# A selective-scan and expert kernel on one core: further rows of longer blocks finished later, the last block in one piece, the first two chunks begun with the first tokens

## The chip, the cores and the metric

The kernel runs on one core of a Trainium2 chip (trn2). The metric is the device time of one execution in microseconds; where several executions were taken, the median. Engines are named as the profile names them: PE (TensorE; PEld its weight loads), DVE (VectorE), ACT (ScalarE), POOL (GpSimd), SP (SyncE, which issues DMAs).

## The reference, cut to what matters

One layer over 4096 tokens of 256 features: a Mamba-like mixer, a layer norm, a mixture of eight experts of which each token uses one, and another layer norm.

```
xz = x @ W_in                                  # 256 -> 2 x 512
convolved = silu(conv4(xz[:, :512]) + conv_b)  # depthwise, 4 taps, causal
x_dbl = convolved @ W_x                        # step size, B (16), C (16)
h[t] = exp(delta*A) * h[t-1] + delta*B*convolved[:, :16]   # scan over tokens
y = (sum(h*C) + convolved*D_param) * silu(xz[:, 512:])
x1 = layernorm(x + y @ W_out)
e = argmax(x1 @ Wr.T + br)                     # one of 8 experts per token
out = layernorm(x1 + relu(x1 @ W1[e].T + b1[e]) @ W2[e].T + b2[e])
```

Everything is float32.

## The kernel before

**First stage.** The tokens go in eight chunks of 512 (loop over `k` at the end of `mamba_moe`). For a chunk, `project(i, c)` (L740) is called for c = 0 to 7: it multiplies 128 columns of W_in (the tile `win`) with the chunk's tokens (`xTb`, features on partitions) into a PSUM bank `pm`, two matmuls over the two halves of the features. ACT evicts it: for c below 4 as `xc` and as `acc` (the first tap with its bias), and DVE adds three more taps (`taps`, L733, L736); silu gives `cv`. For c of 4 to 7 silu gives the gate `sg`. Between the projections of a chunk stand steps of the chunks before: `gauge`, `gauge_out`, `scan`, `gate`, `look`, `look_out`, `project_out`, `choose`, `rank`, `place`. These end in x1, written to DRAM (`x1d`), and in lists that sort the tokens by expert.

**The first DMAs.** Chunk 0's tokens come in two halves of 256 (`first = TB // 2`, L155). For each half SP loads the first 128 features, ACT's queue the other 128 (L162, L163); behind each half SP loads columns of `win` with `columns` (L159): 0 to 127 after the first half, 128 to 511 after the second, 512 to 1023 later (L169). Behind them on SP's queue stand the router weights `wr` (L173), the next chunk's tokens (L142) and smaller weights (`load_later`, L183). In `project(0, 0)` the products are made for the two token halves apart, so that the first can begin early; every other `project` takes 512 tokens at once. PE first turns an identity twelve times (L202), with nothing to compute. `router_weights` (L468), behind `project(0, 2)`, multiplies `wr` with ones into `pw` (L471); DVE makes `mean` of it (L476) and takes it from `wr` (L477), which the router's products `prx` (L894) then use.

**Second stage.** `blocks()` (L693) is a generator over 32 blocks of 128 tokens of one expert; the loop calls `expert(n)` to take n quarters of a block into PE's order, at first between steps of the first stage, then alone. A block `b` has a row gather (`xg`, by `prefetch`, two blocks ahead) and, where the expert changes, a weight load (`we`, 128 x 4360, three buffers), both indirect DMAs of POOL (L502, L520). Then `turn` (L543) transposes the rows into `xgT`; `hidden(b, 0)` and `hidden(b, 1)` (L562) make 8 x 128 hidden features: products `ph` (L577), then bias and relu into `hT`, the first half by ACT (L586), the second by DVE (L588); `close(b, 0)` and `close(b, 1)` (L592) make the output products `pe` (L628) from `hT`. `finish(b)` (L647) adds the rows and the output bias (`xs`, L605, then `r`, L650), and `layernorm` (L251) makes `y`: bn_stats (L256), bn_aggr (L258), square root on ACT (L260), reciprocal (L261), scale (L262). `scatter(b)` (L661) writes the rows of `y` to the output with an indirect DMA of POOL (L663), called in the next block's turn.

**Longer blocks.** Blocks 17, 20, 23, 26 and 29 (`LONG`) take 32, 32, 32, 64 and 64 further rows of their expert (`more_of`). The hidden products run over 160 or 192 columns; for the outputs of the further rows `close(b, 1)` has products of its own, `pf` (L639), split over 4 or 2 groups of partitions. `finish(b)` then does for them what it does for the main rows: `xs` (L656), the sum of the groups (L658), and `layernorm` with the names `stf`, `mvf`, `sdf`; all these rows lie in the tile called `long`. `scatter(b)` writes main and further rows one after the other.

**The last block.** For b = 31 `close` makes the 256 output columns in two halves of 128: all eight products for columns 0 to 127, then sum (L621) and statistics (L622) of that half, then the same for the other, both in one PSUM bank `pe`.

**Seldom blocks.** A loop for up to seven blocks beyond 32 (`seldom`, L671) stands behind block 28 and is skipped when not needed; gathers and scatters of its rows (`seldom`) are always issued by POOL.

**What sets the order.** PE's order is the order written here (`manual_schedule`). The other engines' order is made by a scheduler from the dependences and its own estimates, except where `issue_after` pins a step. A DMA on SP's or ACT's queue takes one of eight semaphores in turn and waits for the DMA that held it before.

Of the kernel before, what the change touches and what calls it, by code (L numbers as in the profile page):

```python
# [37 lines left out]
F32 = mybir.dt.float32  # L38
# [4 lines left out]
ALU = mybir.AluOpType  # L43
# [4 lines left out]
P = 128  # L48
# [3 lines left out]
TB = 512  # L52
# [47 lines left out]
def mamba_moe(  # L100
# [57 lines left out]
    def columns(at):  # L158
        nc.sync.dma_start(win[:, :, at], W_in[:, at].rearrange("(c p) n -> p c n", p=P))  # L159

    for at in (slice(0, first), slice(first, TB)):
        nc.sync.dma_start(st[0]["xTb"][:, 0, at], xT[0:P, at])  # L162
        nc.scalar.dma_start(st[0]["xTb"][:, 1, at], xT[P : 2 * P, at])  # L163
        columns(slice(0, P) if at.start == 0 else slice(P, DI))
    cw = const.tile([P, CC, KC], F32, name="cw")
    nc.scalar.dma_start(cw, conv_w.rearrange("(c p) k -> p c k", p=P))
    cb = const.tile([P, CC], F32, name="cb")
# [80 lines left out]
        allow_small_or_imprecise_dtypes=True,  # L248
    )

    def layernorm(pool, rows, done, name, st=None):  # L251

        n = rows.shape[0]
        if st is None:
            st = pool.tile([P, 6], F32, tag="st", name=f"st{name}")[0:n, :]
            nc.vector.bn_stats(st, rows)  # L256
        mv = pool.tile([P, 2], F32, tag="mv", name=f"mv{name}")[0:n, :]
        nc.vector.bn_aggr(mv, st)  # L258
        sd = pool.tile([P, 1], F32, tag="sd", name=f"sd{name}")[0:n, :]
        nc.scalar.activation(sd, mv[:, 1:2], AF.Sqrt, bias=eps[0:n, :])  # L260
        nc.vector.reciprocal(sd, sd)  # L261
        nc.vector.tensor_scalar(done, rows, mv[:, 0:1], sd, ALU.subtract, ALU.mult)  # L262
# [232 lines left out]
    xgs, wes, turned, hid, last, open_, ys = {}, {}, {}, {}, {}, {}, {}  # L495


    xgf, openf, yf, ends_, wide_, xss, seldom_in, halves = {}, {}, {}, {}, {}, {}, [], []
    current = 0

    def gather(to, rows, at):
# [90 lines left out]
    def close(b, half):  # L592
        we, hT = wes[b], hid[b]
        if half == 0:
            open_[b] = bank("o", f"pe{b}")
        py = open_[b]

        def out_weights(fc):
            return we[:, O2 + fc * D : O2 + (fc + 1) * D]

        def add_rows():
            xss[b] = m2.tile([P, D], F32, tag="xs", name=f"xs{b}")

            with tc.issue_after(last[b].ins):
                nc.vector.tensor_tensor(xss[b], xgs[b], we[:, OC : OC + D], ALU.add)  # L605

        if b == SURE - 1:


            at = slice(half * D // 2, (half + 1) * D // 2)  # L610
            for fc in range(FC):
                nc.tensor.matmul(
                    py[:, at], lhsT=hT[:, fc, :], rhs=out_weights(fc)[:, at],
                    start=(fc == 0), stop=(fc == FC - 1),
                )
            if half == 0:
                add_rows()
                halves.append(m2.tile([P, D], F32, tag="r", name=f"r{b}"))
                halves.append(a2.tile([P, 2, 6], F32, tag="sta", name=f"st{b}"))
            r, sts = halves  # L620
            nc.vector.tensor_tensor(r[:, at], py[:, at], xss[b][:, at], ALU.add)  # L621
            nc.vector.bn_stats(sts[:, half, :], r[:, at])  # L622
            if half == 1:
                ys[b] = m2.tile([P, D], F32, tag="y", name=f"y{b}")
                layernorm(m2, r, ys[b], f"m{b}", sts)
            return
        for fc in range(half * FC // 2, (half + 1) * FC // 2):
            nc.tensor.matmul(  # L628
                py[:, 0:D], lhsT=hT[:, fc, 0:P], rhs=out_weights(fc),
                start=(fc == 0), stop=(fc == FC - 1),  # L630
            )
# [11 lines left out]
        add_rows()  # L643
        if b != SELDOM:
            finish(b)

    def finish(b):  # L647
        we, py, xs = wes[b], open_[b], xss[b]
        r = m2.tile([P, D], F32, tag="r", name=f"r{b}")
        nc.vector.tensor_tensor(r, py[:, 0:D], xs, ALU.add)  # L650
        ys[b] = m2.tile([P, D], F32, tag="y", name=f"y{b}")
        layernorm(m2, r, ys[b], f"m{b}")
        if b in LONG:
            m = more_of(b)
            xs, r, yf[b] = (ends_[b][0:m, n * D : (n + 1) * D] for n in (1, 2, 3))
            nc.vector.tensor_tensor(xs, xgf[b], we[0:m, OC : OC + D], ALU.add)  # L656
            for g in range(0, P, m):
                nc.vector.tensor_tensor(r, openf[b][g : g + m, 0:D], r if g else xs, ALU.add)  # L658
            layernorm(m2, r, yf[b], f"f{b}")

    def scatter(b):  # L661
        for rows, at in ((ys[b], index[b][1]), *(((yf[b], further[b][0 : more_of(b), :]),) if b in LONG else ())):
# [70 lines left out]
    def taps(i, c):  # L733
        acc, xc = st[i]["acc", c], st[i]["xc"]
        for k in range(KC - 1):
            nc.vector.scalar_tensor_tensor(  # L736
                acc, xc[:, c, k : k + TB], cw[:, c, k : k + 1], acc, ALU.mult, ALU.add
            )

    def project(i, c):  # L740
# [10 lines left out]
        pm = bank("mm", f"pm{i}_{c}")  # L751

        for at in (slice(0, first), slice(first, TB)) if i == c == 0 else (slice(0, TB),):
            for dc in range(DC):
                nc.tensor.matmul(  # L755
                    pm[:, at], lhsT=win[:, dc, c * P : (c + 1) * P], rhs=xTb[:, dc, at],
                    start=(dc == 0), stop=(dc == DC - 1),
                )
        if c >= CC:
            evicted = nc.scalar.activation(sg[:, c - CC, :], pm, AF.Silu)  # L760
        else:
            nc.scalar.copy(xc[:, c, KC - 1 :], pm)  # L762
            acc = a3.tile([P, TB], F32, tag="acc", name=f"acc{i}_{c}")
            evicted = nc.scalar.activation(  # L764
                acc, pm, AF.Identity, scale=cw[:, c, KC - 1 : KC], bias=cb[:, c : c + 1]
            )
            s["acc", c] = acc
            if c < CC - 1:
                taps(i, c)
        if ("acc", c - 2) in s:  # L770

            with tc.issue_after(evicted.ins):
                nc.scalar.activation(cv[:, c - 2, :], s["acc", c - 2], AF.Silu)
        if c == CC and i + 1 < NB:

            after = st[i + 1]["xc"] = a2.tile(
                [P, CC, KC - 1 + TB], F32, tag="xc", name=f"xc{i + 1}"
            )
            nc.gpsimd.tensor_copy(after[:, :, 0 : KC - 1], xc[:, :, TB : TB + KC - 1])
# [428 lines left out]
```

## Time and profile before

| | us |
|---|---|
| median of three runs | 487.88 |
| lowest, highest of them | 486.55, 489.39 |
| the profiled execution | 486.12 |
| its span in the profile | 484.4 |
| PE busy in it | 471.3 |
| DVE, ACT, POOL busy | 340.3, 224.0, 185.9 |
| HBM read and written | 87.45 MB, 9.54 MB |

The 1.7 us between the profiled execution and its span lie outside the instructions. The first stage's products run from 4.6 us; from 345 us on only blocks of the second stage are left; the last block's products begin at 470.4 us, and the last scatter is issued at 480.5 us. The granted PE clock is 0.996 of full speed over the span.

How to read the rows: a timeline row has the start in us from the span's start, the length, the engine (a q behind it: its queue of issues), the line, the operation, the tiles written and read, the shape, how many instructions were merged, and in brackets the idle time of the engine before it with what ended it. A busy PE is not a PE at its peak, since ends of matmuls are modelled from starts. Each f32 matmul appears as two records.

### The profile page before, as it was taken

Reading aid. Unit: us, or ns where it says so; the run is one execution under the profiler, and the core shown is the slowest. Engines: PE = TensorE matmul, PEld = TensorE weight load, DVE = VectorE, ACT = ScalarE, POOL = GpSimd, SP = SyncE. Lnnn points to the kernel's source line nnn. Section 1 sums busy time; section 2 is a strip of 40 time slices with the busy share of each in tenths; the row PEclk is TensorE's granted clock in tenths of the full one; section 3 lists DMA queues with packets and bytes.
Section 4 is the critical chain, followed back from the end, with each engine's and each line's share of the span. In section 5 each row is a group of like instructions: output and inputs, shape, how many; then the busy total and the mean of one; then the engine's idle time right before and its main releaser. Section 6 shows DMA issues by size and latency. Waiting matters only on the chain. (4 is left out here: it accounts for less than half of the span.)

```text
span 484.4 us, 7580 instructions
## 1 busy us (share of the span) xinstructions
PE 471.3 (97%) x2618; PEld 352.9 (73%) x2618; DVE 340.3 (70%) x1117; ACT 224.0 (46%) x453; POOL 185.9 (38%) x194
## 2 busy tenths in 40 slices
PE   8999999999999999999999999999999999999984
PEld 5444555546464676777898999999989898889874
DVE  2587969798998997877799779445464645555343
ACT  3777768878878865848443132212111112122111
POOL 2001212444437454241514332535344456644621
PEclk9999999999999999999999999999999999999998
DMA  7501012130407918414677767999874399769700
GB/s 226 171 2 45 0 45 87 43 88 0 132 1 295 391 42 283 158 50 175 184 271 269 278 215 267 387 354 343 344 281 162 87 350 283 229 219 336 275 16 22
DMA packets 23049, 89.65 MB, mean 185 GB/s; under 512 B 4898, under 2 KB 14629, under 8 KB 19298
## 3 DMA queue, kind: packets, MB, share of 16 engines
q0 software_dynamic: 8672, 74.38, 42.2%
q1 hardware_dynamic: 13378, 14.50, 9.5%
q8 instruction: 21, 0.34, 0.3%
q10 hardware_dynamic: 960, 0.27, 0.3%
q14 instruction: 18, 0.15, 0.1%
HBM read 87.45 MB, written 9.54 MB: 200 GB/s over the span
## 5 line engine op out<-in xcount | busy, mean ns | idle before, releaser
L755 PE MATMUL pm<-xTb,win 128*128 128x512 f32 (+1 forms) x260 | 121.3, 597 | 0.2 <-DMA win<-in_W_in 0.2
L577 PEld LDWEIGHTS ph<-xgT,we 128*128 128x128 f32 x864 | 100.9, 192 | 6.3 <-issue 2.8
L577 PE MATMUL ph<-xgT,we 128*128 128x128 f32 x864 | 103.4, 276 | 0.6 <-issue 0.6
L628 PE MATMUL pe<-we,hT 128*128 128x256 f32 x416 | 96.1, 381 | 1.4 <-ACT hT L586 1.0
L628 PEld LDWEIGHTS pe<-we,hT 128*128 128x128 f32 x416 | 76.7, 190 | 11.9 <-ACT hT L586 1.2
L736 DVE SCALAR_TENSOR_TENSOR acc<-xc,cw,acc 128x512 f32<-128x512 f32 x96 | 72.9, 780 | 16.0 <-ACT acc L764 15.6
L755 PEld LDWEIGHTS pm<-xTb,win 128*128 128x128 f32 x260 | 47.6, 192 | 47.0 <-issue 40.9
L260 ACT ACTIVATE sdm<-mvm,eps 128x1 f32<-128x1 f32 x32 | 9.5, 296 | 143.7 <-DVE mvm L258 118.7
L520 POOL DMA_INDIRECT we<-in_experts,widx x32 | 33.7, 1054 | 90.5 <-DVE r L650 25.3
L921 PE MATMUL po<-wout,sg 128*128 128x264 f32 x256 | 64.1, 392 | 0.0
L885 POOL TENSOR_TENSOR sg<-cv,sg 128x512 f32<-128x512 f32 x22 | 32.8, 1495 | 59.3 <-DVE cv L880 45.9
L921 PEld LDWEIGHTS po<-wout,sg 128*128 128x128 f32 x256 | 46.1, 190 | 10.1 <-issue 2.9
L663 POOL DMA_INDIRECT out<-y,tidx x32 | 32.8, 1024 | 35.8 <-DVE y L262 23.4
L588 DVE TENSOR_SCALAR hT<-ph,we 128x128 f32<-128x128 f32 x108 | 31.4, 342 | 20.3 <-issue 8.8
L650 DVE TENSOR_TENSOR r<-pe,xs 128x256 f32<-128x256 f32 x31 | 13.1, 422 | 44.2 <-PE pe L628 37.7
L502 POOL DMA_INDIRECT xg<-x1d,tidx x32 | 32.1, 1004 | 31.0 <-DVE xd L811 7.5
L586 ACT ACTIVATE hT<-ph,we 128x128 f32<-128x128 f32 x108 | 30.7, 367 | 21.1 <-PE ph L577 14.3
L1009 POOL TENSOR_SCALAR rowh<-lrow,row,code 128x256 f16<-128x256 bf16 x20 | 26.0, 1308 | 27.2 <-DVE row L1001 26.0
L880 DVE SCALAR_TENSOR_TENSOR cv<-cv,dp,py 128x256 f32<-128x256 f32 x64 | 28.6, 471 | 3.4 <-PE py L873 3.4
L760 ACT ACTIVATE sg<-pm 128x512 f32<-128x512 f32 x32 | 19.0, 595 | 18.4 <-PE pm L755 16.0
L762 ACT COPY xc<-pm 128x512 f32<-128x512 f32 x32 | 18.6, 582 | 18.0 <-PE pm L755 17.8
L764 ACT ACTIVATE acc<-pm,cb,cw 128x512 f32<-128x512 f32 x32 | 25.1, 784 | 0.0
(224 smaller groups left out, 619.4 us busy)
## 6 DMA issues: line engine op xcount, KB each, us to landing
xb<-in_x SPq DMA_DIRECT2D x8, 512.0 KB, 6.2
x1d<-x SPq DMA_DIRECT2D x8, 512.0 KB, 6.0
xTb<-in_xT SPq DMA_DIRECT2D x7, 512.0 KB, 6.1
win<-in_W_in SPq DMA_DIRECT2D x1, 512.0 KB
we<-in_W_outT SPq DMA_DIRECT2D x1, 512.0 KB
wout<-in_W_out SPq DMA_DIRECT2D x1, 512.0 KB
we<-in_experts,widx POOLq DMA_INDIRECT x32
xg<-x1d,tidx POOLq DMA_INDIRECT x32
```

Of the source, the lines that this page charges most:

```text
L502: nc.gpsimd.indirect_dma_start(out=to, out_offset=None, in_=x1d[0:rows, :], in_offset=bass.IndirectOffsetOnAxis(ap=at, axis=0),)
L520: nc.gpsimd.indirect_dma_start(out=wes[n][:, :], out_offset=None, in_=experts, in_offset=bass.IndirectOffsetOnAxis(ap=weights[n], axis=0), ...
L577: nc.tensor.matmul(ph[:, n * w : (n + 1) * w], lhsT=we[:, at : at + P], rhs=xgT[:, dc * w : (dc + 1) * w], start=(dc == 0), stop=(dc == DC ...
L586: nc.scalar.activation(hT[:, fc, :], ph[:, n * w : (n + 1) * w], AF.Relu, bias=bias)
L588: last[b] = nc.vector.tensor_scalar(hT[:, fc, :], ph[:, n * w : (n + 1) * w], bias, 0.0, ALU.add, ALU.max)
L628: nc.tensor.matmul(py[:, 0:D], lhsT=hT[:, fc, 0:P], rhs=out_weights(fc), start=(fc == 0), stop=(fc == FC - 1),)
L663: moved = nc.gpsimd.indirect_dma_start(out=out, out_offset=bass.IndirectOffsetOnAxis(ap=at, axis=0), in_=rows, in_offset=None, bounds_chec ...
L736: nc.vector.scalar_tensor_tensor(acc, xc[:, c, k : k + TB], cw[:, c, k : k + 1], acc, ALU.mult, ALU.add)
L755: nc.tensor.matmul(pm[:, at], lhsT=win[:, dc, c * P : (c + 1) * P], rhs=xTb[:, dc, at], start=(dc == 0), stop=(dc == DC - 1),)
L880: nc.vector.scalar_tensor_tensor(cv[:, c, at], cv[:, c, at], dp[:, c : c + 1], py[:, 0 : TB // 2], ALU.mult, ALU.add,)
L885: eng.tensor_tensor(sg[:, c, :], cv[:, c, :], sg[:, c, :], ALU.mult)
L921: nc.tensor.matmul(po[:, 0 : D + NE], lhsT=sg[:, c, j * P : (j + 1) * P], rhs=wout[:, c, :], start=(c == 0), stop=(c == CC - 1),)
```

## The change

Three edits.

1. `columns(slice(0, P))` and `columns(slice(P, 2 * P))` are both loaded behind the first token half, and columns 256 to 511 behind the second. `project(0, 0)` makes the products of the first 256 tokens for chunks of columns 0 and 1 into two banks, then those of the second 256 tokens for columns 0; `project(0, 1)` those of the second 256 tokens for columns 1.
2. `finish` keeps the main rows alone. The further rows' `xs` is written in `close(b, 1)`, and the rest is a new function `finish_further`, called for block b - 1 behind `hidden(b, 1)`. Their scatter is called one block later, behind the next block's main scatter.
3. The case of the last block goes: it is closed and finished as every other, in one piece of 256 columns.

```diff
         nc.scalar.dma_start(st[0]["xTb"][:, 1, at], xT[P : 2 * P, at])
-        columns(slice(0, P) if at.start == 0 else slice(P, DI))
+        if at.start == 0:
+            columns(slice(0, P))
+            columns(slice(P, 2 * P))
+    columns(slice(2 * P, DI))
...
-        if b == SURE - 1:
-            at = slice(half * D // 2, (half + 1) * D // 2)
-            for fc in range(FC):
-                nc.tensor.matmul(
-                    py[:, at], lhsT=hT[:, fc, :], rhs=out_weights(fc)[:, at],
-                    start=(fc == 0), stop=(fc == FC - 1),
-                )
-            if half == 0:
-                add_rows()
...
-            nc.vector.tensor_tensor(r[:, at], py[:, at], xss[b][:, at], ALU.add)
-            nc.vector.bn_stats(sts[:, half, :], r[:, at])
-            if half == 1:
-                ys[b] = m2.tile([P, D], F32, tag="y", name=f"y{b}")
-                layernorm(m2, r, ys[b], f"m{b}", sts)
-            return
...
+        if b in LONG:
+            nc.vector.tensor_tensor(
+                ends_[b][0 : more_of(b), D : 2 * D], xgf[b], we[0 : more_of(b), OC : OC + D],
+                ALU.add,
+            )
...
+    def finish_further(b):
         if b in LONG:
             m = more_of(b)
             xs, r, yf[b] = (ends_[b][0:m, n * D : (n + 1) * D] for n in (1, 2, 3))
-            nc.vector.tensor_tensor(xs, xgf[b], we[0:m, OC : OC + D], ALU.add)
             for g in range(0, P, m):
                 nc.vector.tensor_tensor(r, openf[b][g : g + m, 0:D], r if g else xs, ALU.add)
             layernorm(m2, r, yf[b], f"f{b}")
...
             if 0 < b:
                 scatter(b - 1)
+                scatter(b - 2, False)
...
             hidden(b, 1)
+            finish_further(b - 1)
             yield
...
+        if i == 0 and c < 2:
+            if c == 0:
+                for n in range(2):
+                    products(n, slice(0, first))
+            products(c, slice(first, TB))
+        else:
+            products(c, slice(0, TB))
+        pm = banks.pop(c)
```

`products(c, at)` is the pair of matmuls of `project` for one chunk of columns and the tokens `at`; `scatter(b, False)` writes the further rows of block b alone.

More of the change, by code (lines that the diff above doesn't have):

```diff
@@ L249, in mamba_moe, with layernorm @@
     )
-    def layernorm(pool, rows, done, name, st=None):
+    def layernorm(pool, rows, done, name):
         n = rows.shape[0]
-        if st is None:
-            st = pool.tile([P, 6], F32, tag="st", name=f"st{name}")[0:n, :]
-            nc.vector.bn_stats(st, rows)
+        st = pool.tile([P, 6], F32, tag="st", name=f"st{name}")[0:n, :]
+        nc.vector.bn_stats(st, rows)
         mv = pool.tile([P, 2], F32, tag="mv", name=f"mv{name}")[0:n, :]
@@ L495, in mamba_moe @@
     xgs, wes, turned, hid, last, open_, ys = {}, {}, {}, {}, {}, {}, {}
-    xgf, openf, yf, ends_, wide_, xss, seldom_in, halves = {}, {}, {}, {}, {}, {}, [], []
+    xgf, openf, yf, ends_, wide_, xss, seldom_in = {}, {}, {}, {}, {}, {}, []
     current = 0
@@ L599, in out_weights @@
             return we[:, O2 + fc * D : O2 + (fc + 1) * D]
[L601 to L605, printed above, removed]
-        if b == SURE - 1:
-            at = slice(half * D // 2, (half + 1) * D // 2)
-            for fc in range(FC):
-                nc.tensor.matmul(
-                    py[:, at], lhsT=hT[:, fc, :], rhs=out_weights(fc)[:, at],
-                    start=(fc == 0), stop=(fc == FC - 1),
-                )
-            if half == 0:
-                add_rows()
[L618 to L621, printed above, removed]
-            nc.vector.bn_stats(sts[:, half, :], r[:, at])
-            if half == 1:
-                ys[b] = m2.tile([P, D], F32, tag="y", name=f"y{b}")
-                layernorm(m2, r, ys[b], f"m{b}", sts)
-            return
         for fc in range(half * FC // 2, (half + 1) * FC // 2):
@@ L642, in close @@
                 )
-        add_rows()
+        xss[b] = m2.tile([P, D], F32, tag="xs", name=f"xs{b}")
+        with tc.issue_after(last[b].ins):
+            nc.vector.tensor_tensor(xss[b], xgs[b], we[:, OC : OC + D], ALU.add)
+        if b in LONG:
[3 more added lines that the diff above has]
+            )
         if b != SELDOM:
@@ L659, in finish, with scatter @@
             layernorm(m2, r, yf[b], f"f{b}")
-    def scatter(b):
-        for rows, at in ((ys[b], index[b][1]), *(((yf[b], further[b][0 : more_of(b), :]),) if b in LONG else ())):
+    def scatter(b, main=True):
+        rows_at = ((ys[b], index[b][1]),) if main else ()
+        if not main and b in LONG:
+            rows_at = ((yf[b], further[b][0 : more_of(b), :]),)
+        for rows, at in rows_at:
             moved = nc.gpsimd.indirect_dma_start(
@@ L738, in taps @@
             )
+    banks = {}
     def project(i, c):
@@ L750, in project, with products @@
         xc, cv, sg = s["xc"], s["cv"], s["sg"]
-        pm = bank("mm", f"pm{i}_{c}")
-        for at in (slice(0, first), slice(first, TB)) if i == c == 0 else (slice(0, TB),):
+        def products(c, at):
+            if c not in banks:
+                banks[c] = bank("mm", f"pm{i}_{c}")
             for dc in range(DC):
                 nc.tensor.matmul(
-                    pm[:, at], lhsT=win[:, dc, c * P : (c + 1) * P], rhs=xTb[:, dc, at],
+                    banks[c][:, at], lhsT=win[:, dc, c * P : (c + 1) * P], rhs=xTb[:, dc, at],
                     start=(dc == 0), stop=(dc == DC - 1),
                 )
+        if i == 0 and c < 2:
[6 more added lines that the diff above has]
+        pm = banks.pop(c)
         if c >= CC:
```

## The prediction

> **What bounds the kernel now.** I read first the busy shares and the split by stretches of the span, then who TensorE waited for, then the timeline at the two ends and around the last longer block.
>
> ```profile
> PE 471.3 (97%) x2618; PEld 352.9 (73%) x2618; DVE 340.3 (70%) x1117; ACT 224.0 (46%) x453; POOL 185.9 (38%) x194
> ```
>
> TensorE (PE) is the bound: 471.3 of 484.4 us. Between 24 and 345 us it is busy 318.83 of 321 us, between 345 and 458 us 111.89 of 113. So only three places can give anything: the first 12 us, the last 20, and the few waits left between. The list of TensorE's waits (line, releaser, us in total, times, longest):
>
> ```profile
> PE idle L202 <- POOL ident masks.py:199: 1.6, 1, 1.6
> PE pe L628 <- ACT hT L586: 1.0, 1, 1.0
> ...
> PE ph L577 <- issue: 0.6, 2, 0.4
> ...
> PE pe L628 <- DVE hT L588: 0.4, 1, 0.4
> ...
> PE pe L612 <- DVE r L621: 0.4, 1, 0.4
> ```
>
> All its idle time sums to about 7 us. Of this the change can touch: 1.0 + 0.6 us after block 29 (a longer block), 0.4 us after block 23 (the longer block whose products end at 407 us), 0.4 us in the last block, and what the start loses.
>
> **Part 1: the first two chunks.** Weight loads (PEld) show the start best (start us, length, what, idle before):
>
> ```profile
> 4.57 1.35 PEld L755 LDWEIGHTS pm<-xTb,win 128*128 128x128 f32 x4 [0.52 <-issue]
> 6.66 0.73 PEld L755 LDWEIGHTS pm<-xTb,win 128*128 128x128 f32 x4 [0.73 <-DMA xTb<-in_xT]
> 7.75 0.30 PEld L755 LDWEIGHTS pm<-xTb,win 128*128 128x128 f32 x2 [0.37 <-DMA win<-in_W_in]
> 8.29 0.19 PEld L755 LDWEIGHTS pm<-xTb,win 128*128 128x128 f32 x1 [0.24 <-issue]
> ```
>
> An f32 matmul is two records (I say passes). Chunk 0's first 256 tokens take four passes from 4.60 (4.60, 5.16, 5.58, 6.01 in the trace, 0.43 apart), then TensorE waits for the second 256 tokens until 6.66, then four passes 0.22 apart, then a wait for the further columns until 7.75; chunk 2 begins at 9.58. Pass spacings once running: 0.216 us at 256 columns, 0.43 at 512 (rows 8.29, 8.72, 9.15), so four passes of 256 and two of 512 cost the same; the extra weight loads hide (PEld 73%).
>
> After the change chunk 1's first 256 tokens fill the first wait. They need columns 128 to 255, a DMA now of its own, third on SP's queue. If it has landed: first half of chunk 0 over at 6.3 (four passes of 0.43), chunk 1's half 0.32 + 3 x 0.216 = 0.97 to 7.27 (0.32 is the first step after 6.66), two second halves of 4 x 0.216 to 9.00: chunk 2 starts at 9.00 instead of 9.58, -0.58. From the other side: that DMA now stands in the queue where the second 256 tokens stood, released at 6.66; then chunk 2 starts at 6.66 + 0.97 + 1.73 = 9.36, -0.22. If the second tokens, now one 128 KB DMA later, come only when the further columns came (7.75): 7.75 + 1.73 = 9.48, -0.10. I take **-0.45**, near the first: the 128 KB column DMA of now takes 3.2 us from issue to landing, and one issued 0.45 later would be there at 4.9.
>
> What else moves on SP's queue: one issue more (0.4 to 0.5 each), so everything behind stands later. The remaining 256 columns must wait until the first DMA of their semaphore is done, so are issued at about 3.6 (now 2.23); now's 384 KB took 7.75 - 2.23 = 5.5, so by 9.1 at the latest, just when chunk 2 needs them at 9.00; their 256 KB should be sooner. The router weights (wr) slip about 0.45.
>
> [...]
>
> VectorE's order changes too: the operation "mean", which waits for the products with wr, moves from behind seven taps to behind the first:
>
> ```profile
> 9.20 1.54 DVE L736 SCALAR_TENSOR_TENSOR acc<-xc,cw,acc 128x512 f32<-128x512 f32 x2 [7.78 <-ACT acc L764]
> ...
> 15.06 0.16 DVE L476 TENSOR_SCALAR mean<-pw 128x8 f32<-128x8 f32 x1
> ...
> 15.85 0.17 DVE L477 TENSOR_TENSOR wr<-wr,mean 128x16 f32<-128x16 f32 x1
> 17.03 2.33 DVE L736 SCALAR_TENSOR_TENSOR acc<-xc,cw,acc 128x512 f32<-128x512 f32 x3 [1.02 <-ACT acc L764]
> ```
>
> The products now run at 11.3 to 11.8, so at 10.7 to 11.2 then. Chunk 0 is whole 0.5 later (8.29 for 7.79), its first tap ends at 10.4, and VectorE stands about 0.8 us with eleven taps queued behind. Seven taps of 0.66 (six take 4.06) bring wr at 16.1 to 16.2; TensorE wants it for the router at 16.3 (now 16.98). ScalarE's silu of chunk 0 needs its third tap by 15.0 and gets it at 13.5. It costs 0, with cover of only 0.1 us; gone, each us of VectorE's delay is a us of TensorE's. Later gaps (38.32, 43.34) hang on chains that start from TensorE, and shift with it.
>
> **Part 2: the longer blocks' further rows.** The change writes them after the next block's hidden products. But VectorE's and ScalarE's order is made by a scheduler, and the two built programs show the *same* order there: main rows' y, further rows' sums, statistics, root, y, and then the next block's hT. The root (sdf) keeps standing ahead of ScalarE's hT evictions. Around block 29:
>
> ```profile
> 464.69 0.88 DVE L658 TENSOR_TENSOR long<-pf,long 64x256 f32<-64x256 f32 x2 [3.58 <-remote]
> 466.27 0.30 ACT L260 ACTIVATE sdf<-mvf,eps 64x1 f32<-64x1 f32 x1 [5.80 <-DVE mvf L258]
> 466.47 1.11 ACT L586 ACTIVATE hT<-ph,we 128x128 f32<-128x128 f32 x4
> 466.87 3.72 PE L628 MATMUL pe<-we,hT 128*128 128x256 f32 x16 [0.97 <-ACT hT L586]
> ```
>
> TensorE's 0.97 is this chain: sum, root, hT, products. Its head came 3.58 us late though the products pf had ended at 460.88; after block 26 (same size) it came at 433.94, 0.15 behind pf, and TensorE lost nothing. So the stall is not the order but a late signal of TensorE's. Such signals came late after block 23 too (the sum at 407.71, with pf begun at 405.81) and TensorE lost 0.44 at 413.05. The change leaves them: **0**, with -1.57 (0.36 + 0.24 + 0.97) and -0.44 if they don't recur.
>
> What does move is POOL's queue: four further-row scatters (17, 20, 23, 26; the fifth keeps its place) go behind the next block's scatter, 1.3 us each with the gap, plus one wait less (now 1.10 us at 362.34). Queued behind them are a row gather for two blocks ahead (a block takes 7 to 8 us) and the next weight load, which has idled 1.6 to 4.0 us for the block before; where POOL also gathers seldom rows (423.83, idle 0.9) a load may slip 0.4 us, for weights used 15 us later. 0. Bank tags: the pf bank is held half a block longer, of three; pe of the next block takes the third. 0.
>
> **Part 3: the last block.**
>
> ```profile
> 470.63 0.42 DVE L650 TENSOR_TENSOR r<-pe,xs 128x256 f32<-128x256 f32 x1 [1.61 <-PE pe L628]
> ...
> 472.29 0.41 DVE L262 TENSOR_SCALAR y<-r,mvm,sdm 128x256 f32<-128x256 f32 x1
> ...
> 474.00 1.95 PE L612 MATMUL pe<-we,hT 128*128 128x128 f32 x16
> ...
> 476.33 2.05 PE L612 MATMUL pe<-we,hT 128*128 128x128 f32 x16 [0.38 <-DVE r L621]
> 478.42 0.29 DVE L621 TENSOR_TENSOR r<-pe,xs 128x128 f32<-128x128 f32 x1 [1.81 <-PE pe L612]
> ...
> 479.85 0.41 DVE L262 TENSOR_SCALAR y<-r,mvm,sdm 128x256 f32<-128x256 f32 x1
> ```
>
> Divided, the products last from 474.00 to the second sum at 478.42, because the second half waits for the first half's sum. An undivided block goes from first pass to sum in 3.66 us (361.90 to 365.56, 437.61 to 441.27), so the sum starts at 477.66, 0.76 sooner. Behind it everything is on the path: sum to y is 1.43 divided (478.42 to 479.85), 1.66 undivided (470.63 to 472.29), 0.23 back. **-0.53**. hT's second half (475.31) is there before the ninth pass (475.73), so nothing new waits; bounds -0.4 to -0.6.
>
> **Sum**: -0.45 + 0 - 0.53 = -0.98 on 486.12 (span 484.4 and 1.7 around it), 485.1. The median of the three runs is 487.88, 1.8 higher (486.55 to 489.39); the same share of it, 0.2%, gives **486.9**.
>
> **Rivals.**
> - *The late signal after block 29 goes too* (-0.98 - 1.57 = -2.55, in the median 485.3). For: block 26 has no such wait, the release is "remote", and the change moves POOL's queue nearby. Against: order and waits there are unchanged, signals were late at two places in one profile, and it can't say that the runs of the median had them.
> - *The start gives nothing*, the token half or the columns land late: -0.5, 487.4. For: two bounds near -0.1 and -0.2. Against: 3.2 us to landing.
> - *Slower: wr lands late and "mean" blocks VectorE's queue.* Now wr is asked for at 4.10; behind 512 KB and 0.45 later, it holds TensorE at the products, eleven taps, wr's correction and ScalarE's silus. TensorE itself asks for wr at 10.7, so from there on each us late is a us; it beats the gain of 0.98 if wr lands after 11.7, and at 13.0 costs 2.3 - 0.98 = +1.3, 489.2. Against: now the products at 11.29 did not wait.
> - *The further rows are moved in effect* after all: -0.98 - 0.44 - 0.97, much like the first rival; the built order speaks against it.
>
> **How the numbers follow.** Forecast 0.55; late signal gone (or rows moved) 0.20; start gives nothing 0.15; slower 0.10. A measurement here tells about 0.5% (2.4 us) from no change: the forecast and the third case lie within, the first rival reaches just over the line (485.4), the slower case over it half the time. With the medians' own scatter: faster 0.18, same 0.75, slower 0.07. The range for 8 in 10 takes in -2.55 and +0.5 and the scatter: 484.8 to 488.6.
>
> **What would show it.** Chunk 2's first weight load at 9.0 to 9.4 (right) or after 9.6 (start gives nothing); "mean" after one tap with under 1 us idle, no new TensorE wait at prx; sdf still ahead of hT after every longer block, with TensorE's wait there whenever L658's successor starts late; last block one row of 16 passes, sum 3.66 behind its first, y 1.66 behind that. A wait of TensorE over 1 us between 20 and 458 us would make the prediction wrong.

## The result and the profile after

The changed kernel takes 493.76 us (median of 12 runs, 490.81 to 495.34), the kernel before beside it 487.74 (12 runs, 486.34 to 492.1): a ratio of **1.0111** (95% interval 1.0082 to 1.0139). The forecast was 486.9 (range 484.8 to 488.6), a gain of 0.2%, so it was wrong in sign. The profiled execution took 493.81 us, its span is 492.1 (before 484.4).

The page of the changed kernel: busy time of TensorE, and the clock that it was granted in 40 slices of the span.

```profile
PE 475.2 (97%) x2606; PEld 355.3 (72%) x2606; DVE 339.8 (69%) x1115; ACT 223.7 (45%) x453; POOL 185.4 (38%) x194
...
PEclk9998999999999999999999999999999999799998
```

TensorE is busy 3.9 us longer with 12 records fewer, so some products ran at a lower clock: the slice marked 7 lies at 418 to 431 us. The list of TensorE's waits (releaser, us in total, times, longest) has a new head:

```profile
PE pe L604 <- issue: 4.4, 1, 4.4
PE idle L205 <- POOL ident masks.py:199: 1.6, 1, 1.6
```

The wait of 4.4 us stands ahead of block 25's output products, in a place the change doesn't write about. Timelines of TensorE and ScalarE there:

```profile
416.27 3.73 PE L579 MATMUL ph<-xgT,we 128*128 128x128 f32 x32
...
425.13 6.11 PE L604 MATMUL pe<-we,hT 128*128 128x256 f32 x16 [4.36 <-issue]
...
417.93 0.29 ACT L262 ACTIVATE sdm<-mvm,eps 128x1 f32<-128x1 f32 x1 [4.55 <-DVE mvm L260]
424.71 1.14 ACT L588 ACTIVATE hT<-ph,we 128x128 f32<-128x128 f32 x4 [6.49 <-remote]
```

Block 25's first hidden products end near 418.2 (half of the row at 416.27), and ScalarE, which only has to make hT of them, begins at 424.71. It waited for TensorE's signal, and "remote" is all the profile says of its releaser: neither a late engine nor a late transfer, but a late signal, like the one after block 29 that the prediction left alone. Then the 16 passes take 6.11 us for 3.80 in block 24: the granted clock is at half (0.50 of full speed) from 423.18 to 430.0, for 6.8 us. It falls 2.4 us after the end of TensorE's last product (420.77), inside the wait. Another stretch at half, 3.4 us from 44.3, has no such wait ahead of it: in the 3.4 us before it TensorE waited 0.19. So what halves the clock is not shown; that the first stretch follows from the wait is the author's reading.

What else is on POOL's queue then? In the kernel before (start us, length, what, idle before):

```profile
412.50 1.00 POOL L663 DMA_INDIRECT out<-y,tidx  x1 [0.30 <-DVE sdf L261]
413.81 0.89 POOL L663 DMA_INDIRECT out<-long,tidx  x1 [0.30 <-DVE hT L588]
415.00 0.99 POOL L502 DMA_INDIRECT xg<-x1d,tidx  x1 [0.30 <-issue]
418.04 1.03 POOL L520 DMA_INDIRECT we<-in_experts,widx  x1 [2.05 <-issue]
```

And in the changed kernel:

```profile
410.98 1.10 POOL L522 DMA_INDIRECT we<-in_experts,widx  x1 [2.11 <-issue]
...
414.91 1.00 POOL L652 DMA_INDIRECT out<-y,tidx  x1 [0.31 <-DVE hT L590]
416.21 0.96 POOL L504 DMA_INDIRECT xg<-x1d,tidx  x1 [0.30 <-PE pe L604]
417.55 1.02 POOL L522 DMA_INDIRECT we<-in_experts,widx  x1 [0.37 <-issue]
...
421.44 0.89 POOL L652 DMA_INDIRECT out<-long,tidx  x1 [0.30 <-issue]
422.64 0.99 POOL L504 DMA_INDIRECT xg<-x1d,tidx  x1 [0.30 <-issue]
432.06 1.03 POOL L522 DMA_INDIRECT we<-in_experts,widx  x1 [8.43 <-DVE r L635]
```

Before, six indirect DMAs stand in a row from 408.62 (0.3 us between two), then POOL stands 2.05 us: the load, for block 27, goes into the buffer of block 24's weights, and the profile names nobody, but TensorE's signal that block 24's products are done is what it needs. After, block 23's further rows (`out<-long`) are no longer ahead of the row gather, the load finds its signal there, and ten indirect DMAs follow one another from 410.98 to 423.63. ScalarE's hT is let go 1.1 us after the last of them. The other place where the profile before has ten in a row is 450.1 to 462.9, and the late signal after block 29 comes just behind it, at 464.7.

That pause of before was itself made by a late signal. Block 24's last products, and VectorE's sum of them, before and after:

```profile
413.05 1.99 PE L628 MATMUL pe<-we,hT 128*128 128x256 f32 x8 [0.44 <-DVE hT L588]
417.27 0.43 DVE L650 TENSOR_TENSOR r<-pe,xs 128x256 f32<-128x256 f32 x1 [2.84 <-PE ph L577]
...
412.63 3.80 PE L604 MATMUL pe<-we,hT 128*128 128x256 f32 x16
416.79 0.42 DVE L635 TENSOR_TENSOR r<-pe,xs 128x256 f32<-128x256 f32 x1 [0.97 <-PE pe L604]
```

Before, the sum begins 2.2 us behind the end of the products (415.04), and the load 0.8 behind that; after, 0.4 us behind it (416.43). The products end 6.4 us after the run's start before, 5.4 after.

The ends gained about what was forecast. The last block in one piece:

```profile
482.21 3.62 PE L604 MATMUL pe<-we,hT 128*128 128x256 f32 x16
...
485.87 0.42 DVE L635 TENSOR_TENSOR r<-pe,xs 128x256 f32<-128x256 f32 x1 [2.00 <-PE pe L604]
...
487.53 0.41 DVE L264 TENSOR_SCALAR y<-r,mvm,sdm 128x256 f32<-128x256 f32 x1
```

3.66 us to the sum and 1.66 from there to y: 5.32 where the divided block had 5.85. At the start TensorE begins the products with wr at 10.96 (before 11.29), and wr is corrected without harm:

```profile
11.51 0.17 DVE L478 TENSOR_SCALAR mean<-pw 128x8 f32<-128x8 f32 x1 [0.80 <-PE pw L473]
...
16.22 0.17 DVE L479 TENSOR_TENSOR wr<-wr,mean 128x16 f32<-128x16 f32 x1
```

### The profile page after: what moved, and what is told of

Its sections match the earlier page's. It is cut to its first block, busy times and chain, and to the rows that moved or that the text cites. A ratio compares the mean times of both kernels' runs of the same rounds, so it can differ in the third digit from the quotient of the medians.

```text
span 492.1 us, 7552 instructions
## 1 busy us (share of the span) xinstructions
PE 475.2 (97%) x2606; PEld 355.3 (72%) x2606; DVE 339.8 (69%) x1115; ACT 223.7 (45%) x453; POOL 185.4 (38%) x194
## 5 line engine op out<-in xcount | busy, mean ns | idle before, releaser
L749 PE MATMUL pm<-xTb,win 128*128 128x512 f32 (+1 forms) x264 | 122.8, 598 | 0.0
L604 PE MATMUL pe<-we,hT 128*128 128x256 f32 x432 | 102.0, 388 | 5.2 <-issue 4.4
L604 PEld LDWEIGHTS pe<-we,hT 128*128 128x128 f32 x432 | 81.3, 194 | 16.7 <-issue 4.5
L749 PEld LDWEIGHTS pm<-xTb,win 128*128 128x128 f32 x264 | 48.9, 194 | 46.2 <-issue 40.3
L579 PE MATMUL ph<-wide,we 128*128 128x160 f32 (+1 forms) x160 | 24.6, 311 | 1.0 <-DVE r L635 0.7
```

Source lines behind the costliest of these rows:

```text
L579: nc.tensor.matmul(ph[:, n * w : (n + 1) * w], lhsT=we[:, at : at + P], rhs=xgT[:, dc * w : (dc + 1) * w], start=(dc == 0), stop=(dc == DC ...
L604: nc.tensor.matmul(py[:, 0:D], lhsT=hT[:, fc, 0:P], rhs=out_weights(fc), start=(fc == 0), stop=(fc == FC - 1),)
L749: nc.tensor.matmul(banks[c][:, at], lhsT=win[:, dc, c * P : (c + 1) * P], rhs=xTb[:, dc, at], start=(dc == 0), stop=(dc == DC - 1),)
```

## The experiments

Chips differ here, so each group names its chip, a letter in the order of use, and the median of the kernel before on it. B and F bear the same number on record, so they may be one chip; that of the first pair is not on record.

### Which edit it is: chip A, before 487.26 us

Each edit alone, and a control that adds instructions to TensorE's stream without moving anything else. Two theories stood against each other: the stall follows from POOL's new order (only the further rows' edit has it), or from any shift of TensorE's instructions to other places in its stream.

The start alone:

```diff
-        columns(slice(0, P) if at.start == 0 else slice(P, DI))
+        if at.start == 0:
+            columns(slice(0, P))
+            columns(slice(P, 2 * P))
+    columns(slice(2 * P, DI))
...
+            if c == 0:
+                for n in range(2):
+                    products(n, slice(0, first))
+            products(c, slice(first, TB))
```

> The kernel before with the first edit alone (first two chunks begun with the first tokens). Shift theory: TensorE starves around block 25 because the two extra products at the start move every later TensorE instruction to another place in its instruction stream; then this kernel shows most of the loss, ratio 1.007 to 1.012, and a wait of some 4 us of TensorE near 420 us. Queue theory: the four further-row scatters moved on GpSimd's queue cause it; then this kernel is 0.999, the 0.33 us that the start gains in the trace of after. [...]

Measured 0.9967 (0.9948 to 0.9986).

The further rows alone; in the built program only the places of four scatters on POOL's queue differ from the kernel before:

```diff
             if 0 < b:
                 scatter(b - 1)
+                scatter(b - 2, False)
...
+            finish_further(b - 1)
```

> The kernel before with the second edit alone; in the built program it differs from before only in GpSimd's order (four scatters one block later). Queue theory: ratio 1.007 to 1.012 and the wait near 420 us. Shift theory: 1.000, within 0.003, since TensorE's, VectorE's and ScalarE's orders are those of before.

Measured **1.0103** (1.0072 to 1.0133): about as much as the whole change loses. The head of its waits of TensorE:

```profile
PE pe L628 <- issue: 3.5, 1, 3.5
```

It is again ahead of block 25; POOL has ten in a row from 409.50 to 422.31, and ScalarE's hT begins at 422.37:

```profile
422.37 1.14 ACT L586 ACTIVATE hT<-ph,we 128x128 f32<-128x128 f32 x4 [5.74 <-remote]
```

The last block alone:

```diff
-        if b == SURE - 1:
-            at = slice(half * D // 2, (half + 1) * D // 2)
...
-            return
```

> The kernel before with the third edit alone (last block undivided). Both theories: 0.999, the 0.5 us that the end gains in the trace of after; nothing before 470 us changes.

Measured 0.9971 (0.9949 to 0.9993). The three edits alone add up to 1.004, but the whole change gave 1.0111 and, below, 1.0100: whether its stall costs more with the other two edits, or the chips differ in it, stays open.

The control, the second chunk's first product split in two as well:

```diff
-        for at in (slice(0, first), slice(first, TB)) if i == c == 0 else (slice(0, TB),):
+        for at in (slice(0, first), slice(first, TB)) if i == 0 and c < 2 else (slice(0, TB),):
```

> The kernel before with the products of chunk 1 split into two token halves, in their old place and with the old DMAs: two matmuls more in TensorE's stream, nothing else. Shift theory: ratio 1.007 to 1.012, as with the whole change. Queue theory: 1.000, within 0.002. [...]

Measured 1.0006 (0.9985 to 1.0026): the theory of a shift falls.

### Shorter and longer runs: chip B, before 487.70 us

A memset on POOL cuts the run in the kernel with the further rows' edit:

```diff
+    def pause(behind):
+        with tc.issue_after(behind.ins):
+            return nc.gpsimd.memset(win, 0.0)
...
-                gather(xgs[n], *index[n])
+                moved = gather(xgs[n], *index[n])
+                if n == 27:
+                    moved = paused[0] = pause(moved)
```

> The kernel before with the further rows' edit alone, as in the run that cost 1.0103, and one more instruction on POOL: a memset of 2048 columns (estimate 1.7 us, from 0.36 us for 320 columns) between the row gather for block 27 and the weight load for block 27. It writes a buffer that nothing reads any more. Theory of the run: what holds TensorE back is that POOL issues ten indirect DMAs in a row (409.5 to 422.3 us, 0.3 us between them); from about 5.8 us after such a run begins, TensorE's signals to the other engines arrive only some 1 us after the run's end. The memset cuts it into 6 and 5, so ScalarE's hT of block 25 starts on time or at most 1.5 us late: ratio to the kernel before 0.999 to 1.004, TensorE's wait ahead of block 25's output products under 1.5 us. Rival, a late transfer: POOL's queue gets 1.7 us later still, so the loss stays or grows: 1.010 to 1.014. Rival, the register load of the total on TensorE's queue: nothing changes, 1.010.

Measured 1.0037 (1.0019 to 1.0055). POOL and ScalarE:

```profile
415.64 0.96 POOL L506 DMA_INDIRECT xg<-x1d,tidx  x1 [0.31 <-PE pe L637]
416.60 1.83 POOL L503 MEMSET win<- 128x2048 f32 x1
418.59 1.03 POOL L529 DMA_INDIRECT we<-in_experts,widx  x1 [0.17 <-ACT hT L595]
...
417.88 1.14 ACT L595 ACTIVATE hT<-ph,we 128x128 f32<-128x128 f32 x4 [0.20 <-PE ph L586]
```

Block 25's hT comes 0.20 us behind its root for 5.74. What remains is a new wait of 1.1 us for block 26's hT, where POOL, now uninterrupted, runs nine in a row from 418.6 to 430.0. A delay of a transfer would have grown with the memset, so that rival falls, and so does the register load, which is still there.

The other way round, the kernel before with its run made longer, nothing of the change in it:

```diff
+                if n == 27:
+                    for to in spares:
+                        with tc.issue_after(moved.ins):
+                            moved = gather(to, index[n][0], index[n][1][0:32, :])
```

> The kernel before, its further rows where they were, with four more gathers of 32 rows each on POOL, between the row gather and the weight load for block 27; nobody reads what they gather. In the kernel before POOL stands there for 2.05 us and so ends a run of six indirect DMAs at 416.0. Theory of the run: the run now goes on to some 421 us, TensorE's last signal of block 24 arrives about 422.4 for 417.24, ScalarE's hT of block 25 follows it, and TensorE waits 3 to 5 us ahead of block 25's output products: ratio 1.006 to 1.011. Rival, that moving the further rows' scatter makes some transfer late: that scatter is not moved here, 0.999 to 1.003. Rival, the register load of the total: 1.000.

Measured **1.0235** (1.0207 to 1.0264), more than twice what was expected. POOL's wait ahead of the weight load went as well, so the run has 14 members, 408.9 to 426.4: the signal that the load needs came inside the run, as VectorE's sum of block 24 shows, 2.2 us behind its products (415.36). ScalarE and TensorE stood until after the run:

```profile
417.61 0.43 DVE L660 TENSOR_TENSOR r<-pe,xs 128x256 f32<-128x256 f32 x1 [2.86 <-PE ph L587]
...
429.07 1.14 ACT L596 ACTIVATE hT<-ph,we 128x128 f32<-128x128 f32 x4 [10.02 <-remote]
429.49 5.47 PE L638 MATMUL pe<-we,hT 128*128 128x256 f32 x16 [8.85 <-ACT hT L596]
```

The four gathers bring 32 rows of 1 KB each, 128 KB in all. So few bytes speak for the number of DMAs that POOL issues as the cause; no run tells number and bytes apart.

The two good edits, of the start and the last block, in one kernel without the further rows':

> The kernel before with the start's edit and the last block's edit, without that of the further rows. Alone they gave 0.9967 and 0.9971. If they add up, 0.994 (0.992 to 0.996), some 484.5 us where the kernel before has 487.3. Theory of the run: no stall ahead of block 25's output products, the one after block 29 (1.57 us in all) as before. A theory in which the two edits share one gain: 0.997.

Measured 0.9949 (0.9932 to 0.9966). And with two memsets in the run at 450 us:

```diff
-                scatter(n)
+                with tc.issue_after(chain[-1].ins) if chain else nullcontext():
+                    moved = scatter(n)
+                chain.append(pause(moved) if len(chain) in (1, 4) else moved)
```

> The same with two memsets of 2048 columns on POOL among the scatters of the seldom blocks, which in every profile so far stand in one run of ten indirect DMAs (450.1 to 462.9 us in the kernel before). Theory of the run: this run is what makes VectorE's sum after block 29 come 3.3 to 3.6 us late in all six profiles; cut in three it costs nothing, TensorE's 0.36, 0.24 and 0.97 us around block 30 go, and the ratio is 0.003 below that of the same kernel without the memsets: 0.991. Rival, that the branch ahead of block 29 or the matmuls themselves are late there: the sum stays 3.3 us late, ratio as without the memsets, 0.994.

Measured **0.9926** (0.99 to 0.9951), some 1.1 us below the same without memsets (the intervals overlap). The late sum after block 29 is gone; it starts with VectorE's queue, not behind a signal:

```profile
460.04 2.03 DVE L265 TENSOR_SCALAR y<-r,mvm,sdm 128x256 f32<-128x256 f32 x1
462.00 0.86 DVE L647 TENSOR_TENSOR long<-pf,long 64x256 f32<-64x256 f32 x2
```

### A chip that does not do it: chips C, D and E, before 484.56, 484.28 and 484.82 us

Three further questions, on chip C. First, does block 23's scatter alone matter? It goes back behind its y, the other three stay moved:

```diff
-                scatter(b - 2, False)
+                if b - 2 != 23:
+                    scatter(b - 2, False)
...
+            if b - 1 == 23:
+                scatter(23, False)
```

> The kernel before with the further rows' edit, but the scatter of block 23's further rows put back right behind its y, where the kernel before has it; the scatters of blocks 17, 20 and 26 stay moved, one block later. Theory of the run: only block 23's scatter matters, because there POOL's wait ahead of the weight load for block 27 (2.05 us) is what ends a run of six; with it back, no run of more than six indirect DMAs but the one at 450 us, ScalarE's hT of block 25 on time, ratio 0.998 to 1.002. Rival, that each moved scatter costs something or that another block's move is the cause: 1.003 to 1.010.

Measured 1.0002 (0.9978 to 1.0026). Second, does the whole change gain once its runs are cut? The changed kernel with four memsets:

```diff
-                gather(xgs[n], *index[n])
+                moved = gather(xgs[n], *index[n])
+                if n in (27, 28):
+                    moved = paused[0] = pause(moved)
...
+                chain.append(pause(moved) if len(chain) in (1, 4) else moved)
```

> The changed kernel whole, all three edits, with four memsets of 2048 columns on POOL: ahead of the weight loads for blocks 27 and 28, and two among the scatters of the seldom blocks. Theory of the run: what is lost by the further rows' edit is lost by runs of ten indirect DMAs alone; cut to six at most, the edit itself costs nothing, and the ratio is that of the two good edits with the seldom scatters cut, 0.993 (0.991 to 0.996), some 17 thousandths below the changed kernel's 1.011. With a remaining run the loss is up to 0.003 more. Rival, that the edit costs by itself: 1.000 or more.

Measured 0.9981 (0.9959 to 1.0002). Third, do plain DMAs on POOL count as well? The kernel with the longer run, with the four gathers replaced:

```diff
-                            moved = gather(to, index[n][0], index[n][1][0:32, :])
+                            moved = nc.gpsimd.dma_start(to, x1d[0:32, :])
```

> The run that gave 1.0235 with four gathers of 32 rows, but with four plain DMAs of the same size from the same DRAM array, still on POOL's queue and at the same place; nobody reads what they bring. If it is the issue of DMAs by POOL, of any kind, that holds TensorE's signals back: again 1.015 to 1.025. If only the indirect ones do, the plain ones count as a pause: 0.999 to 1.006, with TensorE's wait ahead of block 25's output products under 2 us.

Measured 1.0016 (0.9997 to 1.0035). None of these three tells what it was made for: on this chip no profile shows a late signal anywhere, not even behind ten indirect DMAs at 450 us, and the kernel before is 3 us faster. So the control, the further rows' edit alone, was run beside the same three kernels on yet another chip.

> Control, again the kernel before with the further rows' edit alone. In the call before this one no profile, of any kernel, showed a single late signal of TensorE, not even behind the run of ten at 450 us, and the kernel before itself was 3 us faster there; so the hold-back seems to belong to some chips only. Theory of the run, on a chip that shows it (VectorE's sum after block 29 over 3 us late): 1.010 (1.007 to 1.014), ScalarE's hT of block 25 over 5 us late. On a chip that doesn't show it: 0.999 to 1.002. Rival, that the two have nothing to do with each other: 1.010 on every chip.

Measured 0.9995 (0.9967 to 1.0024) on chip D: the same program that lost 1.03% on chip A loses nothing. Its waits of TensorE have neither line of block 25 or 30:

```profile
PE idle L202 <- POOL ident masks.py:199: 1.6, 1, 1.6
PE pt L863 <- ACT rx L916: 0.7, 1, 0.7
PE ph L577 <- DVE r L659: 0.7, 1, 0.7
```

Around block 25 this program has no run of ten here: POOL stands 1.29 us ahead of the weight load, between two runs of five. So the loss could not come there. That the chip holds nothing back shows at the other place: ten in a row from 449.50 to 462.31, and VectorE's sum after block 29 begins within the run, 0.15 us behind its products (460.24):

```profile
415.19 1.02 POOL L520 DMA_INDIRECT we<-in_experts,widx  x1 [1.29 <-issue]
...
460.39 0.87 DVE L668 TENSOR_TENSOR long<-pf,long 64x256 f32<-64x256 f32 x2
```

Block 23's scatter back:

> As p2_not23, beside its control. Theory of the run: 0.998 to 1.002 on either sort of chip, but now it tells something only if the control loses 1 per cent. Rival, another block's moved scatter is the cause: as the control.

Measured 0.9995 (0.9968 to 1.0022).

All edits and four memsets:

> As after_pauses, beside its control: the whole change with the runs of POOL's indirect DMAs cut by four memsets. Theory of the run: 0.991 to 0.996 on a chip that shows the hold-back (the kernel before then pays for the run at 450 us, this one doesn't), 0.996 to 1.000 on one that doesn't. Rival, that the edit of the further rows costs by itself: 1.000 or more where the control loses.

Measured 0.997 (0.9944 to 0.9996).

Four plain DMAs:

> As b_plain4, beside its control: four plain DMAs on POOL where four gathers gave 1.0235. If any DMA that POOL issues holds the signals back: 1.015 to 1.025 on a chip that shows the hold-back; if only indirect ones do: 0.999 to 1.006.

Measured 1.0009 (0.998 to 1.0039). Chip D shows no late signal either, and again these three decide nothing. One more try with block 23's scatter back, on chip E:

> As p2_not23, once more, in the hope of a chip that shows the hold-back; its own profile is the control: the run of ten at 450 us makes VectorE's sum after block 29 over 3 us late there, and the kernel before takes 487 us for 484. Theory of the run, on such a chip: with block 23's scatter back in place 0.998 to 1.002, where the whole edit gave 1.0103. Rival, another block's moved scatter is the cause: 1.003 to 1.010. On a chip without the hold-back it tells nothing.

Measured 0.9977 (0.996 to 0.9994), again without late signals. Its profile says something else: POOL has ten in a row at the same place (407.55 to 420.1), since here its weight load never waits, and yet

```profile
416.04 1.14 ACT L586 ACTIVATE hT<-ph,we 128x128 f32<-128x128 f32 x4 [0.40 <-PE ph L577]
```

ScalarE starts in time. A run of ten did nothing on this chip.

### The changed kernel with its runs cut, side by side: chip F, before 486.41 us

The changed kernel as it is:

> The changed kernel as it is. On a chip that shows the hold-back (VectorE's sum after block 29 over 3 us late in this profile): 1.008 to 1.014 again, with TensorE waiting 3 to 5 us ahead of block 25's output products. Theory of the run, on a chip that doesn't: the further rows' edit costs nothing, the two ends' gains remain, 0.994 to 0.998. Rival, that the whole change is slower for a cause of its own: above 1.003 on every chip.

Measured **1.0100** (1.0074 to 1.0125).

The same with the four memsets:

> The same with the four memsets that cut POOL's runs. Theory of the run: 0.991 to 0.996 on a chip that shows the hold-back, where the kernel without them loses 1 per cent; on one that doesn't, the same as the kernel without them within 0.002. Rival, that memsets help or cost by themselves: over 0.003 apart on a chip without the hold-back.

Measured **0.9937** (0.9913 to 0.9962), all three edits and four memsets in it. The head of TensorE's waits in the first, again ahead of block 25's output products:

```profile
PE pe L604 <- issue: 3.7, 1, 3.7
```

And POOL, TensorE and ScalarE around block 25 in the second:

```profile
415.99 1.83 POOL L505 MEMSET win<- 128x2048 f32 x1
417.98 1.03 POOL L533 DMA_INDIRECT we<-in_experts,widx  x1 [0.16 <-ACT hT L599]
...
419.54 3.72 PE L615 MATMUL pe<-we,hT 128*128 128x256 f32 x16
...
417.27 1.14 ACT L599 ACTIVATE hT<-ph,we 128x128 f32<-128x128 f32 x4 [0.20 <-PE ph L590]
```

On one chip, the change loses 1.0% as it is and gains 0.6% when nothing but memsets is added to POOL's queue. Block 25's output products then start at once. This and the kernel with the two good edits and two memsets (0.9926, chip B) both beat the kernel before and the changed one; which of the two is better the runs don't tell.

## Why the prediction was wrong

*Start, forecast -0.45 us (bounds -0.58 to -0.10)*: right in size, -0.33 in the first profile (10.96 for 11.29), -0.39 in the second (chip F), but not for the reason given for a value near the larger bound. The extra DMA of columns was to be there at 4.9; TensorE waited for it until 6.39, so what came was the forecast's view "from the other side", a little earlier than its 6.66:

```profile
6.39 3.05 PEld L749 LDWEIGHTS pm<-xTb,win 128*128 128x128 f32 x14 [0.64 <-DMA win<-in_W_in]
```

Alone it measured 0.9967, that is -0.7 to -2.5 us; the part beyond 0.4 was not located. VectorE stood 0.80 us at "mean", as forecast, and wr came at 16.22.

*Last block, forecast -0.53*: right, 5.32 for 5.85. Alone 0.9971, -0.3 to -2.5 us. Both ends together gave -1.7 to -3.3 us on chip B; on chips C and D the kernel with all edits and memsets gave -0.9 and -1.5, near the forecast's -0.98.

*Further rows, forecast 0*: **this is the step that failed**, and in one sentence of it. That VectorE's and ScalarE's order stays was right, and so was that only POOL's queue moves. But "four further-row scatters ... go behind the next block's scatter" was priced by who is queued behind them (a gather, a weight load, both with time to spare), and came out as 0. What the queue's order also decides is where POOL pauses. The pause of 2.05 us ahead of the weight load at 418.04 ended a run of six; with the change it was gone, and the run had ten members. In the second profile (chip F), which is free of the 1.6 us that the first loses to a half-rate clock at 44.3 us (four passes of 512 columns take 3.61 us there for 1.98), the path against that of the kernel before reads: -0.3 us ahead of block 25; 3.8 lost by its late signal; 1.5 more by output products at a lower clock (5.19 us for 3.72; the slice of the granted clock there is marked 8); -0.5 in the last block; and 488.8 - 484.4 = 4.4 in the span. What took the pause away is not settled: one scatter of 0.9 us no longer stands ahead of the load, and the run begins later against block 24's products, whose signal then came in time. On chip E, where no signal is late, there is no such pause even with the scatter in its old place. The prediction counted such idle time of POOL as time to spare; here it was the trace of a late signal.

*Late signal after block 29 goes too (a rival, chance 0.20)*: it did not go, but it was the clue. The prediction saw the 3.58 us, saw "remote", saw that "the change moves POOL's queue nearby", and asked only whether that signal would improve. It did not ask what had made it late, and so whether the change could make a second one. The ten scatters ahead of it stand in the same profile. With that question a loss could have stood among the rivals; as it was, the only rival on the slow side was one of the start.

*"A wait of TensorE over 1 us between 20 and 458 us would make the prediction wrong"*: it was there, 4.36 us.

What is shown: of the three edits, that of the further rows brings the loss (alone 1.0103). It comes by the long run: cut by memsets on one chip, 1.0100 becomes 0.9937, and a longer run without the edit loses more (1.0235). And it comes on some chips alone (A, B, F and that of the first pair): on E a run of ten at the same place held nothing back, on C and D the one at 450 us didn't. What is only argued or open:

- Whether block 23's scatter alone does it, or an earlier one that shifts the run against TensorE's products: the run made for that fell on chips C, D and E.
- Whether plain DMAs on POOL hold signals back (tried only on C and D), and whether the DMAs' number or their bytes count.
- Why some chips hold signals and others don't. All executions here were recorded, with a span and a clock, and the records differ: the traces of the first pair hold 1056 and 1035 landing signals of POOL's DMAs, and their pages, that of the further rows' edit on A and both of F give no time to landing for POOL's DMAs, while the page of the same edit on D gives 10.0 us for the weight loads and 6.5 for the row gathers. That the recording has a part in it is the author's guess: no run here shows it, and no unrecorded execution was seen.

## What to carry to other kernels

Before an edit that moves DMAs on one queue is priced at nothing, list that queue's uninterrupted runs before and after, and not only what stands behind the moved one: a wait that looks like waste can be what breaks a run, and can itself come from a late signal. A late "remote" release in the profile before (3.58 us here) was a mechanism at work; find what precedes it at every place where it occurs, and ask whether the change makes another. And when a loss of 1% turns up, repeat the control on each chip together with the experiments, or an experiment may fall where there is nothing to measure.

## What the runs showed of the hardware that was not expected

- On chips A, B, F and that of the first pair, TensorE's signals to other engines come late while POOL issues indirect DMAs with 0.3 us between them. A run of six made one 2.2 us late (417.27 for 415.04) and cost TensorE at most some tenths; ScalarE stood 5.7 to 6.5 us ahead of block 25's hT with runs of nine and ten at 410 us and 10.0 with a run of 14, VectorE 3.3 to 3.6 behind block 29 with the run of ten at 450 us. In the two kernels with a run of ten at 410 us, the last signal in time came 5.7 and 5.8 us after the run began; in the run at 450 us of the kernel before one came in time 8.9 us after its start (the sum at 459.04; 7.4 after the run's one gap over 0.3 us), so no fixed time is shown. ScalarE's hT was let go 0.1 to 2.7 us after the last DMA of the run. VectorE's and ScalarE's signals to each other came in time meanwhile (in the run at 450 us the root, reciprocal and y of block 29's main rows begin at 460.18, 460.50 and 460.70).
- A memset of POOL, 1.83 us, breaks such a run. It is not free: VectorE's y beside one took 2.03 us (at 460.04 above) for 0.41 elsewhere.
- Behind a wait of TensorE of 3.5 to 4.4 us, block 25's output products took 5.19 to 6.11 us for 3.72, another 1.5 to 2.4 us. The granted clock was at half for 6.8 us there in the first profile, and the slice is marked 8 in the two others (the further rows' edit on A, the changed kernel on F).
